# A gated attention kernel on one Trainium2 core: the attention phase with every engine and the DMA queue held to the order of the source

## Chip, cores and metric

The kernel runs on one core of one Trainium2 chip. The metric is the device time of one execution in microseconds (us), as the median of several runs. Five engines work side by side: TensorE (PE in the profile; its weight loads are PEld), VectorE (DVE), ScalarE (ACT), GpSimd (POOL) and SyncE (SP). Each works through its own list of instructions in order and waits on semaphores for the others. Transfers are issued from the lists of SP, ACT or POOL.

## What is computed

Eight sequences x (512 tokens of 256 features, float32) pass four blocks, each added to x with a scalar gate tanh(g), and each reading a layernorm of x:

```
x = x + tanh(g0) * cell(ln(x), ctx, ctx)        # mLSTM cell, 8 heads of 32
x = x + tanh(g1) * ffn0(ln(x))                  # attention, 32 heads of 8, then experts
x = x + tanh(g2) * cross(ln(x), ctx)            # attention, 16 heads of 16, key mask
x = x + tanh(g3) * ffn1(ln(x))                  # product-key experts, 8 heads, top 8 of 4096
```

The cell weighs its scores with exp of cumulated gates, causally. `ffn0` is softmax attention within a sequence, a projection, and for each 256-token half of a sequence one of eight two-layer gelu experts; `cross` is softmax attention over the context. `ffn1` projects, normalises over the whole batch, picks the best keys, and sums gelu(x . down) * weight * up over the chosen experts; the kernel takes the products with all 4096 rows of `down` and picks afterwards.

## The kernel before, in words

There are three phases. The **attention phase** (`attention_phase`) does the first three blocks for all sequences, and next to them the products with `down` for `ffn1`. The short **fold** prepares the key matrix. The **chosen phase** (`chosen_phase`) does the picking and sums; its lists of PE, DVE, ACT and POOL are written by hand.

In the attention phase one Python driver decides the order of PE's list, and a scheduler that sits between the kernel's source and the chip orders the lists of all other engines and of SP by its own estimate. The driver is `run` (line 264). It keeps a `Clock` (line 36): a guess of when PE, DVE, ACT and POOL are done with what has been written so far. In each turn it collects candidates, each with the time from which it may run, takes the first that is ready, or else the earliest, and lets it write its instructions.

* **Half-steps** (`attend`, `half_step`). The two attentions are 48 jobs: 4 of kind A (`ffn0`) and 2 of kind C (`cross`) for each sequence. A job has 8 steps of two half-steps. One half-step writes score products (`sc`, L545) of the job whose row maxima are sought, and together with them score products of the job before it, whose exponentials are taken. DVE reduces the first to maxima (`nm`, L565), ACT takes exp of the second (`pr`, L601 for A, L604 for C). After a step PE multiplies `pr` with the values (`av`, L620). There are two score tiles, so the next half-step waits for DVE's nm and ACT's exp of the one before. 48 jobs x 16 half-steps, with maxima and exponentials side by side, make 768.
* **Slots** (`fill_slot`, L507). Before a job, queries and keys are read from images in DRAM (`im_Aq` and so on, written by `halve`, L459 and L460) into one of three slots: 32 transfers for a job of kind A, 24 for one of kind C, and 4 more of a mask row for each second job of kind C. All are issued on SP.
* **Lane 1** per sequence m: load of X and cT (L304, L306, POOL's queue), `cell` (layernorm `qn`, gates, four pairs of heads; for each pair a broadcast load `mb` of 512 KB, L756, masked by POOL at L775, turned into `pd` by ACT at L784, multiplied by DVE at L798 with the scores `csc`, L791, and summed by PE into `cav`, L766), `queries`, `values0` and `context` (images and values for the jobs).
* **Lane 2** per sequence: `experts` (w1e, w2e and b2e loaded on POOL's queue, L671 to L689; products L940 and L967; gelus L954), `operands`, and after the jobs of kind C `leave`, which stores x and its layernorm and frees X.
* **The down lane** (`inner_products`): for each sequence, once it has left, 32 pieces of four products (`ps_hd`, L209), evacuated to `raw` by ACT or DVE and stored to DRAM.

Candidates of `attend` come first in the list, then lane 2, lane 1 and the down lane; so a lane runs where no half-step, tail or value product is ready. Lane pieces that need PSUM share two banks (`Room`, line 153). A lane ends a piece with `yield t`, the time at which it wants to go on; `("rest", name)` waits for an event, and `("take", ...)` for the one accumulator that cell and experts share. `stats`, `normalize` and `layernorm` (lines 117 to 139) write all of their DVE instructions in one go, and POOL's inverse square root between them.

## Time and profile before

| | us |
|---|---|
| three runs | 4493.82, 4502.52, 4508.36 |
| median | 4502.52 |
| profiled execution, its own time | 4506.63 |
| its span | 4504.9 |
| PE, PEld, DVE, ACT, POOL busy | 3811.9, 2039.0, 2482.6, 1777.3, 773.2 |
| mean granted clock of TensorE | 0.84 |
| first and last nm of a half-step fall into | 160 to 450, 3150 to 3375 |
| last down products and fold | 3375 to 3495 |
| chosen phase | 3495 to 4505 |

The profile is one execution. A busy PE is not PE at its peak: its matrix products are pipelined, and they take about twice the time where the granted clock is 0.5. The idle time of an engine is put down to the one whose semaphore came last.

### The profile page before, as it was taken

The numbers are of one execution on the slowest core, as the hardware profiler recorded it, in microseconds if no ns is written. First come the engines' busy times: TensorE is split into PE (matmuls) and PEld (weight loads), VectorE is DVE, ScalarE is ACT, GpSimd is POOL, SyncE is SP. The second block draws the span as 40 slices with busy tenths as digits, with TensorE's granted clock in tenths as the row PEclk, the third lists the DMA queues.
The fourth block names the chain that finished last, engine by engine and source line by source line (L and its number), as shares of the span: only waits on it lengthen the run. The fifth ranks groups of instructions, "written<-read, shape, count | busy, mean of one in ns | idle before, by whom it ended". The sixth has DMA issues, their size and how long they took to land.

```text
span 4504.9 us, 60683 instructions
## 1 busy us (share of the span) xinstructions
PE 3811.9 (85%) x23237; PEld 2039.0 (45%) x23237; DVE 2482.6 (55%) x5698; ACT 1777.3 (39%) x2382; POOL 773.2 (17%) x998
## 2 busy tenths in 40 slices
PE   5587888789879887997899789898898688888888
PEld 2233434333433442353334334433434466666667
DVE  2555533454445444544443454433332899999997
ACT  2244534354534544453445345444441323322321
POOL 2110100100011001101000100100000444444443
PEclk7677857788878977997888889796898799999999
DMA  2311311223233222332332232231255022222221
GB/s 88 83 50 45 80 40 45 66 87 99 73 79 94 87 68 85 103 82 57 104 94 64 78 92 82 67 117 33 78 173 189 32 84 75 90 89 72 87 88 48
DMA packets 206227, 365.81 MB, mean 81 GB/s; under 512 B 27376, under 2 KB 150544, under 8 KB 201456
## 3 DMA queue, kind: packets, MB, share of 16 engines
q1 hardware_dynamic: 187008, 304.99, 22.2%
q0 software_dynamic: 13824, 48.24, 3.7%
q10 hardware_dynamic: 5104, 8.69, 0.5%
q8 instruction: 184, 3.01, 0.3%
q14 instruction: 107, 0.88, 0.1%
HBM read 248.43 MB, written 113.39 MB: 80 GB/s over the span
## 4 chain that ended last, share of the span: by engine, by line
PE 34%; DVE 24%; ACT 3%; DMA 2%; issue 2%; POOL 2%; SPq 0%; ACTq 0%; POOLq 0%; DVEq 0%
PE sc L545 10%; PE ps_hd L209 8%; PE av L620 5%; DVE m L1466 4%; DVE m L1479 4%; DVE g L1508 3%; DVE nm L565 2%; DVE i L1331 2%; PE ps_p L426 2%; PE ps_y L967 2%; DVE s L1329 2%; PE ps_h L940 1%; ACT pr L604 1%; ACT pr L601 1%; DVE ppk L1331 1%
## 5 line engine op out<-in xcount | busy, mean ns | idle before, releaser
L565 DVE TENSOR_REDUCE nm<-sc 128x2 f32<-128x1024 f32 x768 | 937.8, 1223 | 1117.4 <-PE sc L545 1114.1
L601 ACT ACTIVATE pr<-sc 128x1024 f32<-128x1024 f32 x512 | 523.3, 1022 | 605.7 <-PE sc L545 586.0
L545 PE MATMUL sc<-ks,qs 32*128 32x512 f32 x1536 | 490.6, 580 | 101.1 <-DVE nm L565 74.1
L209 PE MATMUL ps_hd<-dx,dw 128*128 128x512 f32 x1024 | 535.4, 656 | 36.8 <-DMA dx<-xT_d 19.2
L545 PEld LDWEIGHTS sc<-ks,qs 32*128 32x128 f32 x1536 | 187.6, 210 | 687.1 <-issue 382.4
L1516 PE MATMUL acc<-up_sb,g 128*128 128x256 f32 x2048 | 476.8, 386 | 2.1 <-issue 2.1
L545 PE MATMUL sc<-qs,ks 32*128 32x512 f32 x1536 | 422.0, 545 | 36.8 <-DVE nm L565 32.4
L604 ACT ACTIVATE pr<-sc,m_off 128x1024 f32<-128x1024 f32 x256 | 282.6, 1113 | 354.8 <-PE sc L545 354.2
L1516 PEld LDWEIGHTS acc<-up_sb,g 128*128 128x128 f32 x2048 | 381.3, 191 | 63.6 <-issue 15.6
L620 PE MATMUL av<-pr,va 128*32 128x512 f32 x2048 | 336.8, 736 | 75.4 <-ACT pr L601 73.4
L1487 POOL TENSOR_TENSOR m<-m2b,wr 64x512 bf16<-64x512 bf16 x256 | 270.5, 1057 | 521.0 <-DVE m L1479 502.9
L545 PE MATMUL sc<-mx,pick_g 4*128 4x512 f32 x1536 | 353.1, 452 | 0.0
L209 PEld LDWEIGHTS ps_hd<-dx,dw 128*128 128x128 f32 x1024 | 189.9, 203 | 269.9 <-issue 235.8
L176 ACT COPY raw<-ps_hd 128x512 f32<-128x512 f32 x204 | 118.8, 584 | 332.4 <-PE ps_hd L209 316.1
L1499 PE MATMUL cf<-m,m 128*128 128x64 bf16 x6144 | 230.7, 200 | 14.3 <-POOL m L1487 10.6
L1499 PEld LDWEIGHTS <-m 128*128 128x128 bf16 x6144 | 226.2, 103 | 30.3 <-issue 11.5
L620 PE MATMUL av<-pr,vb 128*32 128x512 f32 x1024 | 162.8, 713 | 61.4 <-ACT pr L604 61.4
L671 POOL DMA_DIRECT2D w1e<-in_w x32 | 23.3, 728 | 1069.5 <-PE ps_h L940 1069.5
L545 PEld LDWEIGHTS sc<-qs,ks 32*128 32x128 f32 x1536 | 169.6, 211 | 78.2 <-DVE nm L565 42.1
L775 POOL TENSOR_SCALAR_AFFINE_SELECT mb<-mb 128x256 f32<-128x256 f32 x128 | 52.2, 407 | 876.0 <-DMA mb<-nM_d 484.0
L784 ACT ACTIVATE pd<-mb,aT 128x512 f32<-128x512 f32 (+3 forms) x256 | 131.2, 555 | 180.6 <-PE cav L766 82.6
L1466 DVE TENSOR_TENSOR m<-ml,iota 128x2048 bf16<-128x2048 bf16 x128 | 195.2, 1525 | 0.0
(232 smaller groups left out, 5656.4 us busy)
## 6 DMA issues: line engine op xcount, KB each, us to landing
g_d<-raw SPq DMA_DIRECT2D x128, 512.0 KB
g<-g_d SPq DMA_DIRECT2D x32, 2048.0 KB
dw<-in_down SPq DMA_DIRECT2D x128, 256.0 KB
w1e<-in_w POOLq DMA_DIRECT2D x32, 512.0 KB, 4.2
w2e<-in_w POOLq DMA_DIRECT2D x32, 512.0 KB, 4.6
mb<-nM_d SPq DMA_DIRECT2D x32, 512.0 KB
qs<-im_Aq SPq DMA_DIRECT2D x512, 32.0 KB
ks<-im_Ak SPq DMA_DIRECT2D x512, 32.0 KB
```

Source lines behind the costliest of these rows:

```text
L209: nc.tensor.matmul(ps.tile, dws[i][:, k, u, :], xt[:, k, :], start=(k == 0), stop=(k == NK - 1),)
L545: nc.tensor.matmul(sc[:, i, :], lhs[r : r + rows], rhs[r : r + rows], start=(n == 0), stop=(n == len(terms) - 1),)
L565: nc.vector.tensor_reduce(self.nm[:, c, 2 * half : 2 * half + 2, g], sc, AX.X, ALU.max, negate=True)
L601: nc.scalar.activation(self.pr[jj], sc, AF.Exp, scale=self.scale)
L604: nc.scalar.activation(self.pr[jj], sc, AF.Exp, bias=m_off[:, col : col + 1], scale=self.scale,)
L620: nc.tensor.matmul(self.av[32 * j : 32 * j + 32, :], self.va[:, c, h * (self.hd + 1) : h * (self.hd + 1) + 32], pr[j // 2][:, j % 2, :], s ...
L1331: last = nc.vector.max_index(out=index[:, n, :], in_max=values[:, n, :], in_values=source(n))
L1466: nc.vector.tensor_tensor(m1, at[:, 0].unsqueeze(2).to_broadcast([P, 8, P, 2]), iota.unsqueeze(1).to_broadcast([P, 8, P, 2]), ALU.is_equal,)
L1479: last = nc.vector.tensor_tensor(m2[r, 0:2, :, NJ * d : NJ * d + NJ, :], m2b[r].unsqueeze(1).to_broadcast([64, 2, 8, NJ, 2]), wr[r, u, 0:2 ...
L1487: after(nc.gpsimd.tensor_tensor(m2[r, 2, :, NJ * d : NJ * d + NJ, :], m2b[r], wr[r, u, 2].unsqueeze(2).to_broadcast([64, 8, NJ, 2]), ALU.mult,
L1499: nc.tensor.matmul(cf[:, s, :], m1[:, s // 2, :, s % 2], m2[:, i, s // 2, :, s % 2], start=(i == 0), stop=(i == 2),)
L1516: nc.tensor.matmul(accs[t], gts[t][:, j, :], up_sb[:, j, :], start=(j == 0), stop=(j == NJ - 1))
```

## The change

All five lists of the attention phase (PE, DVE, ACT, POOL, SP) follow the order in which the driver writes the instructions; the scheduler no longer moves any of them. With that the helpers are cut: a new `("side", t)` yield marks a place between two pieces that need no PSUM bank; such pieces are put ahead of everything else that is ready. The driver's times get somewhat longer (0.65 for 0.5 for four transposes, 0.14 more a half-step, 0.08 more for a value product). Transfers issued on POOL's queue are issued on SP's. The setup of constants that PE and POOL began with becomes a lane, `prepare`. The `cell` writes `decay` two blocks ahead of the scores. Images have three buffers, and `values1` is a piece of its own that lane 2 writes after `leave` for sequences 2 and up. Two rules pace the lanes: each half-step adds 1.42 us of credit for lane work on PE, and lane pieces come ahead of the next half-step as long as credit is left; and the down lane is held to a line from 0 pieces at 28% of the half-steps to 195 at their end, ahead of the other lanes when more than 3 pieces behind it, and after the half-steps when not behind it.

The core of the diff (the other places do the same to their lines: `nc.gpsimd.dma_start` becomes `nc.sync.dma_start` for X, cT, w1e, w2e, b2e and cte; callers of the helpers use `yield from`; `side` yields stand between the gate computations):

```diff
+        self.work = 0.0
         self.at = {"dve": 0.0, "act": 0.0, "pool": 0.0}
 
     def mm(self, cost, after=0.0):
         self.pe = max(self.pe, after) + 1.08 * cost
+        self.work += 1.08 * cost
         return self.pe + 0.3
 
...
 
+    def side(t):
+
...
         for c in range(NC):
             nc.vector.bn_stats(st[:, c, :], src[:, c, :])
+            t = ck.on("dve", 0.42, after)
+            if c % 2:
+                yield side(t - 0.5)
         for c in range(NC):
             nc.vector.bn_aggr(mv[:, c, :], st[:, c, :])
+        t = ck.on("dve", 0.6, after)
         inv_sqrt(rs, mv[:, :, 1], EPS_LN)
-        return mv, rs, ck.on("dve", 2.2, after)
+        t = ck.on("pool", 1.5, t)
+        yield side(t)
+        return mv, rs, t
...
+            t = ck.on("dve", 0.4, after)
+            if c % 2 and c < NC - 1:
+                yield side(t - 0.5)
+        return t
...
+            t = self.at if self.side else max(self.at, room())
+            if self.need is not None and (self.need == "prepared" or self.need[1] >= 0):
                 if self.need not in done:
...
+                elif said[0] == "side":
+                    self.side, self.at = True, said[1]
...
-    def run(lanes, others=lambda: []):
+
+    SHARE = 1.42
+    pace = {"credit": 0.0, "part": 0.0, "down": 0}
+
+    def behind():
+
+        return 195 * max(0.0, pace["part"] - 0.28) / 0.72 - pace["down"]
+
+    def run(lanes, down, others):
+
+
+        def piece(lane):
+            def step():
+                before = ck.work
+                lane.step()
+                pace["credit"] -= ck.work - before
+                if lane is down and ck.work > before:
+                    pace["down"] += 1
+
+            return step
 
         while True:
-            cands = others()
+            first, half = [], []
+            for t, step, is_half in others():
+                (half if is_half else first).append((t, step))
+            rest = []
             for lane in lanes:
                 t = lane.when()
                 if t is not None:
-                    cands.append((t, lane.step))
+                    (first if lane.side else rest).append((t, piece(lane)))
+            t = down.when()
+            if t is not None:
+                if behind() > 3:
+                    rest.insert(0, (t, piece(down)))
+                elif behind() > 0 or not half:
+                    rest.append((t, piece(down)))
+                else:
+                    spare = NJ * sum(("left", m) in done for m in range(M)) - pace["down"]
+                    rest.append((max(t, ck.pe + max(0.1, 0.8 - 0.05 * spare)), piece(down)))
+            cands = first + (rest + half if pace["credit"] > 0 else half + rest)
...
-            nc.gpsimd.dma_start(xbs[m], x[b].rearrange("(c p) d -> p c d", p=P))
+            nc.sync.dma_start(xbs[m], x[b].rearrange("(c p) d -> p c d", p=P))
             cTs[m] = cxp.tile([P, NK, S], F32, name="cT", tag="cT")
-            nc.gpsimd.dma_start(cTs[m], cxT[b].rearrange("(k p) s -> p k s", p=P))
+            nc.sync.dma_start(cTs[m], cxT[b].rearrange("(k p) s -> p k s", p=P))
 
...
-        nc.gpsimd.memset(nms.bitcast(F32), 0.0)
...
-        nc.gpsimd.memset(cte, 1.0)
-        for i in range(2):
-            nc.gpsimd.memset(v0s[i], 1.0)
-            nc.gpsimd.memset(v1s[i], 0.0)
-
+        nc.vector.memset(cte, 1.0)
...
-        bo_ps = ps_m.tile([P, S], F32, name="bo_ps", tag="m")
-        for k in range(NK):
-            nc.tensor.matmul(
-                bo_ps[:, :D], bqkv_sb[:, 4 + k : 5 + k].to_broadcast([P, P]), w3_sb[:, 3, k, :],
-                start=(k == 0), stop=(k == NK - 1),
-            )
-        nc.vector.tensor_tensor(tbo, bo_ps[:, :D], tbo, ALU.add)
-        nc.vector.tensor_scalar(tbo, tbo, tg[:, 2:3], None, ALU.mult)
...
+        def prepare():
+
+            yield side(ck.pe + 12.0)
+            for i in range(2):
+                nc.vector.memset(v0s[i], 1.0)
+                yield side(ck.dve(NC * W0 // 2, ck.pe) + 0.5)
+            nc.gpsimd.memset(nms.bitcast(F32), 0.0)
+
+            nc.vector.tensor_reduce(p2, ident.rearrange("p (m g) -> p g m", g=2), AX.X, ALU.add)
+            nc.vector.tensor_copy(pick, p2)
+            yield side(ck.on("dve", 0.5, ck.pe) + 1.0)
+            nc.sync.dma_start(m_u8, mask)
+            yield side(ck.pe + 4.0)
+            m_f = prb.tile([P, 2, S], F32, name="m_f", tag="pr")[: B * NC, 0, :P]
+            nc.vector.tensor_copy(m_f, m_u8)
+            t = ck.on("dve", 0.3, ck.pe)
+            m_neg = prb.tile([P, 2, S], F32, name="m_neg", tag="pr")[: B * NC, 0, :P].bitcast(F32R)
+            nc.vector.tensor_scalar(m_neg, m_f, 1.0, -NEG, ALU.subtract, ALU.mult)
+            nc.sync.dma_start(m_dram, m_neg.bitcast(F32))
+            yield t
+            mp = Room([P, S], "mp", t)
+            nc.tensor.transpose(mp.tile[:, : B * NC], m_f, ident[: B * NC, : B * NC])
+            mp.mm(0.2)
+            nc.vector.tensor_copy(m_key, mp.tile[:, : B * NC])
+            mp.free(ck.on("dve", 0.3, mp.t))
+            nc.vector.tensor_scalar(m_off, m_key, 1.0, -NEG, ALU.subtract, ALU.mult)
+            ck.on("dve", 0.3, mp.t)
+            yield ck.pe + 4.0
+            bo_ps = Room([P, S], "bo_ps")
+            for k in range(NK):
+                nc.tensor.matmul(
+                    bo_ps.tile[:, :D], bqkv_sb[:, 4 + k : 5 + k].to_broadcast([P, P]),
+                    w3_sb[:, 3, k, :], start=(k == 0), stop=(k == NK - 1),
+                )
+            bo_ps.mm(NK * D * F4)
+            nc.vector.tensor_tensor(tbo, bo_ps.tile[:, :D], tbo, ALU.add)
+            bo_ps.free(ck.dve(D, bo_ps.t))
+            nc.vector.tensor_scalar(tbo, tbo, tg[:, 2:3], None, ALU.mult)
+            yield side(ck.dve(D, bo_ps.t) + 2.0)
+            for i in range(2):
+                nc.gpsimd.memset(v1s[i], 0.0)
+                yield side(ck.on("pool", 2.0, ck.pe) + 2.0)
+            done["prepared"] = ck.pe
...
+            t = ck.act(S, ps.t)
+            ps.free(t + 1.5)
+            yield side(t)
+            if bias is None:
                 nc.vector.tensor_tensor(lo, ps.tile, hi.bitcast(F32), ALU.subtract)
             else:
-                nc.scalar.activation(hi, ps.tile, AF.Identity, bias=bias)
-                t = ck.act(S, ps.t)
                 nc.vector.scalar_tensor_tensor(
                     lo, ps.tile, bias, hi.bitcast(F32), ALU.add, ALU.subtract
                 )
-            ps.free(ck.dve(S, t))
+            t = ps.free(ck.dve(S, t))
             nc.sync.dma_start(dst[0, n], hi.bitcast(F32))
+            yield side(t)
             nc.sync.dma_start(dst[1, n], lo.bitcast(F32))
...
-            images[(kind, m)] = drm.tile([2, 2, P, S], F32, name=f"im_{kind}")
+            images[(kind, m)] = drm.tile([2, 2, P, S], F32, name=f"im_{kind}", bufs=3)
...
-            def close_maxima(self):
+            def gather_maxima(self):
                 at = nms.rearrange("p c (j r) -> p c j r", j=4)
                 nc.vector.tensor_copy(at[:, :, :, 0:2], self.nm)
                 nc.vector.tensor_tensor(
                     at[:, :, :, 2:4], self.nm, at[:, :, :, 0:2].bitcast(F32), ALU.subtract
                 )
-                t = ck.on("dve", 0.3, self.reduced)
-                ps = Room([P, S], "nmT", t)
+                self.gathered = ck.on("dve", 0.4, self.reduced)
...
+            def close_maxima(self):
+                ps = Room([P, S], "nmT", self.gathered)
...
-                t = ck.mm(S * F4, there)
+                t = ck.mm(S * F4 + 0.08, there)
...
-                nc.gpsimd.dma_start(
+                nc.sync.dma_start(
...
+            yield side(ck.pe + 2.5)
             for pair in range(4):
                 mb = cel.tile([P, 2, S], F32, name="mb", bufs=1)
                 nc.sync.dma_start(mb, nM_d[2 * pair : 2 * pair + 2].partition_broadcast(P))
-                yield ck.pe + 4.5
+                yield side(ck.pe + 3.0)
...
+                def decay(c):
                     s0 = c * P
                     nc.gpsimd.affine_select(
...
-                    t = ck.on("pool", 0.5, ck.pe)
-                    pd = cel.tile([P, 2, S], F32, name="pd")
+                    t = ck.on("pool", 0.8, ck.pe)
+                    pd = pds[c] = cel.tile([P, 2, S], F32, name="pd")
...
+                    ready[c] = t
+
+                def scored(c):
+                    s0 = c * P
+                    pd = pds[c]
...
@@ -799,12 +874,29 @@
                             pd[:, i, s0:], sc[i].tile[:, s0:], 1.0 / math.sqrt(32.0),
                             pd[:, i, s0:], ALU.mult, ALU.mult,
                         )
-                        t = sc[i].free(ck.dve(S - s0, max(t, sc[i].t)))
-                    if last is not None:
-                        sums(*last)
-                    last = (c, pd, t)
-                    yield 0.0 if c < NC - 1 else t
-                t = sums(*last)
+                        ready[c] = sc[i].free(ck.dve(S - s0, max(ready[c], sc[i].t)))
+
+                def sums(c):
+                    pd = pds.pop(c)
+                    for i in range(2):
+                        h = 2 * pair + i
+                        nc.tensor.matmul(
+                            av[64 * i : 64 * i + 64, c * P :],
+                            cte[:, c, 33 * h : 33 * h + 64],
+                            pd[:, i, c * P :], start=(c == 0), stop=(c == NC - 1),
+                        )
+                    return ck.mm((S - c * P) * F4, ready[c])
+
+                decay(0)
+                yield side(ready[0] - 1.0)
+                decay(1)
+                for c in range(NC):
+                    yield ready[c] - 0.5
+                    scored(c)
+                    yield ready[c]
+                    t = sums(c)
+                    if c + 2 < NC:
+                        decay(c + 2)
                 avs = osb.tile([P, S], F32, name="avs", tag="avs", bufs=1)
                 nc.scalar.copy(avs, av)
                 t = ck.act(S, t)
...
-                t = ht.free(ck.on("dve", 1.2, ht.t))
-            t = layernorm(hk, hk, t)
+                t = ht.free(ck.on("dve", 1.4, ht.t))
+                yield side(t)
...
-            yield ("rest", ("loaded", m - 2, 3, "A"))
+            yield ("rest", ("loaded", m - 3, 3, "A"))
...
-            yield ("rest", ("job", m - 2, 1, "C"))
+
+        def values1(m):
+            b = order[m]
+            yield ("rest", "prepared")
+            cT = cTs[m]
...
-            yield tp
+            yield side(tp - 3.5)
...
+                yield side(max(t, tb))
...
                 yield from context(m)
+                if m < 2:
+                    yield from values1(m)
...
                 yield from leave(m)
+                if m + 2 < M:
+                    yield from values1(m + 2)
...
-                    def close(job=job):
-                        closed[job] = live[job].close_maxima()
-                        st["close"] = None
-                    cands.append((max(live[job].reduced + 0.3, room()), close))
+                    op = live[job]
+                    if op.gathered is None:
+                        cands.append((op.reduced, op.gather_maxima, False))
+                    else:
+                        def close(job=job):
+                            closed[job] = live[job].close_maxima()
+                            st["close"] = None
+                        cands.append((max(op.gathered, room()), close, False))
...
-            t = ck.mm(deep * S * F1)
+            t = ck.mm(deep * S * F1 + 0.14)
+            pace["credit"] = min(pace["credit"] + SHARE, 2 * SHARE)
+            pace["part"] = st["i2"] / (STEPS * len(jobs))
...
-        lanes = [Lane(lane2()), Lane(lane1()), lane_down]
-        run(lanes, attend)
+        lanes = [Lane(lane2()), Lane(lane1()), Lane(prepare())]
+        run(lanes, lane_down, attend)
...
-    with tc.manual_schedule(engines={mybir.EngineType.PE}):
+    with tc.manual_schedule(
+        engines={
+            mybir.EngineType.PE, mybir.EngineType.DVE, mybir.EngineType.Activation,
+            mybir.EngineType.Pool, mybir.EngineType.SP,
+        }
+    ):
```

## The prediction, made before the changed kernel ran

> **What bounds the kernel now.** I read the page's slices first, then the table of stages, then TensorE's waits, then the timelines of single stops. The profiled execution took 4506.63 us with a span of 4504.9 us; the median of the three runs, 4502.52 us, lies 4 us lower, so sums against the span are lowered by 2.4 us at the end.
>
> ```profile
> PE   5587888789879887997899789898898688888888
> DVE  2555533454445444544443454433332899999997
> PEclk7677857788878977997888889796898799999999
> ```
>
> The last ten slices are the chosen phase: DVE is full there, and the change doesn't touch it (3495 to 4505, 1010 us). The first thirty are the attention phase and the short fold. There no other engine is full: TensorE is busy 8 or 9 tenths of the time, but its granted clock swings between 0.6 and 0.9. The stages, as start:end, us, busy us of PE, PEld, DVE, ACT and POOL, granted clock, DMA share, GB/s:
>
> ```profile
> 160.00:450.00 290.00, 224.63 (x1060) 88.32 (x1060) 161.07 (x262) 118.58 (x165) 24.41 (x45) 0.69 0.22 56
> 450.00:900.00 450.00, 370.83 (x1876) 185.57 (x1872) 193.28 (x283) 195.57 (x225) 55.62 (x64) 0.74 0.21 58
> 900.00:1350.00 450.00, 389.80 (x1957) 172.95 (x1956) 210.76 (x321) 207.64 (x266) 43.41 (x62) 0.84 0.30 85
> 1350.00:1800.00 450.00, 392.66 (x2008) 175.52 (x2008) 208.97 (x324) 207.00 (x268) 44.20 (x64) 0.84 0.29 84
> 1800.00:2250.00 450.00, 394.70 (x2032) 181.23 (x2028) 210.42 (x331) 208.31 (x270) 43.81 (x63) 0.86 0.30 86
> 2250.00:2700.00 450.00, 393.35 (x1970) 180.34 (x1968) 207.50 (x340) 199.53 (x256) 47.63 (x65) 0.83 0.29 82
> 2700.00:3150.00 450.00, 407.72 (x2100) 189.03 (x2098) 182.72 (x226) 205.16 (x241) 21.93 (x26) 0.82 0.26 74
> 3150.00:3375.00 225.00, 204.90 (x1120) 101.74 (x1120) 72.89 (x117) 100.64 (x122) 10.82 (x13) 0.93 0.38 122
> ```
>
> These 3215 us hold all 768 half-steps. PE is busy 2778.6 us in sum, so it idles 436 us. Each stage's busy time by its clock gives the work at full clock: 155.0 + 274.4 + 327.4 + 329.8 + 339.4 + 326.5 + 334.3 + 190.6 = 2277 us. The other 501 us of busy time are lost to the low clock. So the stage runs at 2277 / 3215 = 71% of what PE could do, and 937 us are in play. The waits of PE in it (total, times, longest):
>
> ```profile
> PE sc L545 <- DVE nm L565: 106.5, 118, 6.6
> PE ps_t L403 <- DVE qn L132: 77.9, 5, 17.8
> PE av L620 <- ACT pr L601: 73.4, 83, 2.3
> PE av L620 <- ACT pr L604: 61.4, 64, 1.4
> ```
>
> The clock goes with them. Around one wait for qn and in a stretch where the lanes had no work left, the same table reads:
>
> ```profile
> 2101.00:2119.00 18.00, 3.37 (x14) 0.89 (x11) 1.77 (x9) 1.02 (x1) 6.46 (x8) 0.50 0.26 73
> 2119.00:2129.00 10.00, 9.62 (x32) 4.17 (x32) 4.35 (x7) 2.19 (x3) 0.00 (x0) 0.55 0.01 2
> ...
> 3045.00:3056.00 11.00, 7.63 (x59) 2.81 (x57) 4.60 (x5) 4.37 (x6) 0.00 (x0) 1.00 0.31 93
> ...
> 3070.00:3120.00 50.00, 40.87 (x201) 16.22 (x200) 17.50 (x18) 15.53 (x17) 0.00 (x0) 0.50 0.04 11
> ```
>
> After the stop PE works 10 us at half clock. From 3045 on there are only half-steps and values. PE first gets by with 7.63 of 11 us; then the clock falls to 0.50 and stays, with 41 of 50 us busy: a pair of half-steps that took 5.2 us takes 7.2 us in the timeline. So missing filler costs the gap and then the clock.
>
> **The change part by part.** No matrix product is added, so the 2277 us stay; what changes is who waits.
>
> *Loads of X, cT, cte, w1e, w2e, b2e go from POOL's queue to SP's.* At 2110 the load of X stands behind POOL's work for another sequence:
>
> ```profile
> 2109.12 0.91 POOL L923 TENSOR_SCALAR b2e<-b2e,tg 128x256 f32<-128x256 f32 x1 [2.73 <-DMA b2e<-in_b]
> ...
> 2110.77 0.77 POOL L304 DMA_DIRECT2D X<-in_x  x1
> 2115.75 1.41 DVE L123 BATCH_NORM_STATS2 ln_st<-X 128x6 f32<-128x256 f32 x4 [15.04 <-DMA X<-in_x]
> ```
>
> DVE sits in front of its next nm for 15 us, PE with it. On SP the load goes out where lane 1 asks for it, 5 us by the driver before its first reader; its issue-to-landing median is 4.8 us. I count the 77.9 us as gone. What is late next there is the chain statistics, POOL, normalisation, about 6 us, under half-steps. SP pays for 128 more issues at 0.34 us (an mb issue) to 0.9 us (a cte issue on POOL): 44 to 115 us of its own time in 3000, on no path unless something urgent stands behind.
>
> *DVE, ACT, POOL in the order of the source, helpers cut by side yields.* At 1869 to 1875 DVE ran bn_stats, aggregates, two waits of 1.47 us for POOL and four normalisations before one nm whose scores were ready, and PE stood 5.73 us. With the cuts a half-step's nm can go in between. Of the 106.5 us I take half, 53: the 118 waits average 0.9 us, and the short ones are plain latency. The bounds are 0 and 106. The gelus of an expert half are written together: before, 63 table loads at L954 for 32 halves, 55 at L604 and 13 at L601, 1283 ns each; about half go, some 80 us of ACT, which is busy under half of the time, so nothing by itself.
>
> *Credit of 1.42 us a half-step, and the down lane held to a line.* Lane pieces then stand between exponentials and values. Of the 134.8 us of av waits I take half, 67; of the waits for gates (16.7 + 4.0 us), 10. The bounds are again nothing and all. The down products (L209) are missing from 1577-1689, 2365-2477, 2815-2928 and 3040-3153, with clocks of 0.76, 0.81, 0.77 and 0.70 against 0.94 in the slices beside them: (0.18 x 97.5) + (0.13 x 101.6) + (0.17 x 99.3) + (0.24 x 95.2) = 70 us. Spread to 195 pieces over the last 72% they fill these; I take 50, since part is in the next term.
>
> *The new in-order waits.* No row shows them. The nearest: a fill of one A job's slot is 32 SP issues, from 1522.30 to 1537.37, that is about 12 us without its wait, and mb (needed by POOL, then ACT, then the exponentials behind it) can stand behind one. Fills take 48 x 12 = 576 us, a fifth of SP's time, and the mean rest of one is 6 us: 28 loads of mb beside half-steps x 0.2 x 6 = 34 us. With a like share for DVE and ACT I take 60; the ends are 0 and 28 x 12 = 336.
>
> *Start.* PE waits 11.14 us for mp and 18.92 us for bo_ps, and DVE's tbo holds the first layernorm behind it: the first transposes come at 33.62. With `prepare` later they need X and about 6 us of chain: 20 us gained. Three images and values1 in lane 2 only move work; nothing taken. The tail (3375 to 3495: last down, fold) is kept at 120 us.
>
> **The sum.** Idle: -78 - 53 - 67 - 10 + 60 = -148, leaving 288 of 436. The clock's loss follows idle in proportion: 501 x 148 / 436 = -170, and -50 for the down lane. Start: -20. Together -388: 4504.9 - 388 = 4117 us of span, 4115 against the median. The stage then runs at 2277 / (3215 - 368) = 80%; the old kernel's stretch 2690-2810 reaches 106.91 x 0.93 / 120 = 83% and 1465-1577 84%, so this asks for nothing unseen.
>
> Two rules of the Trainium skill speak against parts of this. "TensorE: Matmul & The Clock Gate", section "Why this matters for your kernels", asks only for no idle gaps over about 3 us; yet the stretch at 3070 has none above 0.8 us and stays at 0.50. By the rule only five stops would give clock back (5 x 5 us), not 220 us, and the time would be about 4310; I go by the row. "DMA: Bandwidth & Descriptors", section "Issuing engines are not separate DMA queues", says that the issuing engine saves only sequencer time; what the row at 2110 shows is that sequencer's queue, 12 us of it. By the rule alone the X term falls and the time is some 170 us higher.
>
> **Rivals.**
> 1. *The order hardly differs, or latency is the limit.* For it: most PE waits are under 1 us, and PE was in the driver's order already. Then only the X loads (78 us + 5 x 5 us of clock) and the start (20) go: 4505 - 123 = 4380.
> 2. *SP's single queue stalls the exponentials; slower.* The place is mb behind fills and behind waits for buffers. For it: POOL already waits 484.0 us in 30 pieces for mb, up to 40.3 us, and SP stands 560.9 us at L507 for slots. Against it: those waits cost ACT only 50.2 us, as its order had other work first, and a fill is now issued when the driver says its slot is free. A stop of 12 us costs 12 + 5 of clock; 28 of them 476 us: 4115 + 476 = 4591. It decides once the mean stop passes about 10 us (28 x 14 = 390).
> 3. *The balance starves the lanes*, so that jobs wait for images: a cell alone takes 33 to 111 us at the start; 30 us of that exposed in each of seven sequences takes 210 us back: 4325, still faster.
>
> **How the numbers follow.** Forecast (3880 to 4335, rival 3 in it) 0.66, and 0.04 below; rival 1 (4335 to 4490) 0.10; within 0.3% of 4502, which is about what a measurement tells from no change, 0.03; rival 2 and its like 0.17. The lower end is the best: 2277 / 0.88 = 2587, 628 us less, and 20: 3857, rounded to 3880. The range takes in rival 1 and ends at 4520, leaving out 0.04 below and some 0.15 above. The forecast's own range is 3880 to 4335.
>
> **What would show it.** Right: no wait for qn above 3 us; granted clock near 0.9 in all stages after 450; L209 in every slice from about 0.28 on; few av waits; the last half-step near 2960 instead of 3349. Wrong: ACT pd or POOL mb waits that stand right before PE's stops; DVE waiting for POOL or DMA with nm behind; slices at clock 0.7 that hold L209; or a chosen phase other than 1010 us.

## The result, and the profile after

The kernel after takes 4529.76 us (median of 13 runs, 4512.56 to 4576.2), the kernel before 4495.56 us beside it (13 runs, 4467.67 to 4508.36): ratio 1.008, interval [1.0052, 1.0108]. It is slower, a little; 4115 us were forecast. The profiled execution took 4512.56 us, the fastest of the 13, with a span of 4510.8 us.

In the slices, the full ones at the end are as before. In the first thirty TensorE shows as many sevens and eights as it did:

```profile
PE   5587889889779889987888999788887689888888
PEclk6656869789889788996988989687898799999999
```

The stages of the kernel after (start:end, us, busy us of PE, PEld, DVE, ACT and POOL, granted clock, DMA share, GB/s), some of them, and then the whole stretch:

```profile
160.00:450.00 290.00, 221.55 (x944) 87.23 (x944) 136.85 (x224) 98.80 (x127) 23.56 (x37) 0.62 0.22 51
...
900.00:1350.00 450.00, 377.11 (x1941) 175.35 (x1939) 205.22 (x322) 188.42 (x244) 30.10 (x44) 0.89 0.32 90
1350.00:1800.00 450.00, 402.58 (x2016) 180.40 (x2016) 210.88 (x331) 196.81 (x256) 31.86 (x48) 0.84 0.29 84
...
2700.00:3150.00 450.00, 370.25 (x1904) 175.09 (x1900) 168.59 (x218) 176.65 (x214) 24.95 (x27) 0.80 0.25 72
```

```profile
160.00:3375.00 3215.00, 2736.98 (x14090) 1262.14 (x14090) 1459.52 (x2249) 1341.26 (x1709) 221.20 (x308) 0.83 0.28 80
```

PE idles 3215 - 2737 = 478 us here, where it idled 436. Busy time by clock, stage by stage, is 2278 us: the same work in the same 3215 us, with 459 us lost to the clock in place of 501. The waits of PE (total, times, longest), from the start to the chosen phase:

```profile
PE sc L615 <- DVE nm L635: 141.4, 116, 24.5
PE av L692 <- ACT pr L673: 83.8, 86, 1.2
PE ps_hd L224 <- DVE pd L873: 49.5, 26, 10.0
PE sc L615 <- ACT pr L673: 48.0, 38, 11.1
```

L635 is the nm of L565 before, L615 the scores, L692 the values. The waits for qn are gone (1.6 us in this stretch after 77.9). In their place stand long stops at nm, pd and pr: between 160 and 3375 there are 16 stops of 4 us or more, 174 us in all, where the kernel before had 14 with 134 us. One of 24.47 us ends at 2049.74. SP's list ahead of it:

```profile
2002.78 6.25 SPq L576 DMA_DIRECT2D qs<-im_Aq  x16
2009.30 6.56 SPq L576 DMA_DIRECT2D ks<-im_Ak  x16
2016.00 6.21 SPq L576 DMA_DIRECT2D qs<-im_Aq  x16
2022.25 7.17 SPq L576 DMA_DIRECT2D ks<-im_Ak  x16
2029.77 7.32 SPq L576 DMA_DIRECT2D qs<-im_Aq  x16
2037.23 7.19 SPq L576 DMA_DIRECT2D ks<-im_Ak  x16
2044.60 0.34 SPq L527 DMA_DIRECT2D im_Ck<-pk_h  x1
2045.04 0.38 SPq L529 DMA_DIRECT2D im_Ck<-pk_l  x1
```

and what the other engines do when it is through (the bracket: idle time before, and what ended it):

```profile
2047.08 0.69 ACT L516 ACTIVATE pk_h<-ps_p,bqkv_sb 128x512 fp32r<-128x512 f32 x1 [35.50 <-DMA im_Ck<-pk_h]
2047.80 0.75 DVE L523 SCALAR_TENSOR_TENSOR pk_l<-ps_p,bqkv_sb,pk_h 128x512 fp32r<-128x512 f32 x1 [26.68 <-ACT pk_h L516]
...
2049.74 0.79 PE L615 MATMUL sc<-ks,qs 32*128 32x512 f32 x2 [24.47 <-DVE nm L635]
```

Read upwards: PE waits for an nm, which stands in DVE's list behind a pk_l; that needs a pk_h of ACT; ACT waits 35.5 us for a free pk_h buffer, because the store that frees it (L527) stands in SP's list behind three slot fills. Those are 96 issues and last 42 us. Each piece is where the driver wrote it. The same thing with mb in the place of the store stops PE for 8.81 us at 981.67, behind one fill of kind C that keeps SP from 961.68 to 974.24; here the way leads over POOL's mask and pd:

```profile
970.58 3.66 SPq L576 DMA_DIRECT2D kx<-im_Ck  x8
974.66 0.34 SPq L836 DMA_DIRECT2D mb<-nM_d  x1
...
979.73 0.41 POOL L845 TENSOR_SCALAR_AFFINE_SELECT mb<-mb 128x256 f32<-128x256 f32 x1 [36.01 <-DMA mb<-nM_d]
980.17 1.34 ACT L854 ACTIVATE pd<-mb,aT 128x512 f32<-128x512 f32 x2 [10.85 <-POOL mb L845]
```

And the load of X, which the change put on SP, is itself caught once, behind two fills and four stores:

```profile
164.93 5.37 SPq L576 DMA_DIRECT2D ks<-im_Ak  x16
...
172.25 0.77 SPq L353 DMA_DIRECT2D X<-in_x  x1
178.75 0.75 DVE L129 BATCH_NORM_STATS2 ln_st<-X 128x6 f32<-128x256 f32 x2 [16.44 <-DMA X<-in_x]
...
180.68 0.79 PE L615 MATMUL sc<-ks,qs 32*128 32x512 f32 x2 [17.52 <-DVE nm L635]
```

Sorted by the transfer that comes late, the 174 us are: image stores 66.5 us (three stops of 21 to 24 us), mb or the store nM_d that it reads 55.7 us (six of 7 to 11), X 17.5 us (one), the fills' own keys 22.4 us (four of 5 to 7) and dw, the rows for the down products, 12.2 us (two).

### The profile page after: what moved, and what is told of

The parts are those of the page before. It is cut to its first block, busy times and chain, and to the rows that moved or that the text cites. A ratio compares the mean times of both kernels' runs of the same rounds, so it can differ in the third digit from the quotient of the medians.

```text
span 4510.8 us, 60390 instructions
## 1 busy us (share of the span) xinstructions
PE 3775.1 (84%) x23237; PEld 2027.6 (45%) x23237; DVE 2501.0 (55%) x5742; ACT 1675.8 (37%) x2279; POOL 670.4 (15%) x867
## 5 line engine op out<-in xcount | busy, mean ns | idle before, releaser
L635 DVE TENSOR_REDUCE nm<-sc 128x2 f32<-128x1024 f32 x768 | 934.8, 1222 | 992.9 <-PE sc L615 983.8
L615 PE MATMUL sc<-ks,qs 32*128 32x512 f32 x1536 | 487.2, 587 | 200.8 <-DVE nm L635 138.8
L224 PE MATMUL ps_hd<-dx,dw 128*128 128x512 f32 x1024 | 535.9, 653 | 99.8 <-DVE pd L873 49.5
L615 PEld LDWEIGHTS sc<-ks,qs 32*128 32x128 f32 x1536 | 188.9, 212 | 708.5 <-issue 292.9
L615 PE MATMUL sc<-qs,ks 32*128 32x512 f32 x1536 | 398.7, 536 | 33.1 <-ACT pr L673 24.6
L692 PE MATMUL av<-pr,va 128*32 128x512 f32 x2048 | 347.3, 757 | 84.5 <-ACT pr L673 83.8
L615 PE MATMUL sc<-mx,pick_g 4*128 4x512 f32 x1536 | 335.8, 446 | 0.0
L191 ACT COPY raw<-ps_hd 128x512 f32<-128x512 f32 x171 | 100.3, 587 | 299.9 <-PE ps_hd L224 289.5
L873 DVE SCALAR_TENSOR_TENSOR pd<-csc,pd 128x512 f32<-128x512 f32 (+3 forms) x256 | 115.3, 487 | 167.4 <-PE csc L866 110.1
L615 PEld LDWEIGHTS sc<-qs,ks 32*128 32x128 f32 x1536 | 159.5, 206 | 102.9 <-issue 46.6
L116 POOL TENSOR_SCALAR ln_rs<-ln_mv 128x4 f32<-128x4 f32 x40 | 9.3, 232 | 1211.5 <-DVE ln_mv L134 1211.5
```

The costliest lines, as they stand in the source:

```text
L224: nc.tensor.matmul(ps.tile, dws[i][:, k, u, :], xt[:, k, :], start=(k == 0), stop=(k == NK - 1),)
L615: nc.tensor.matmul(sc[:, i, :], lhs[r : r + rows], rhs[r : r + rows], start=(n == 0), stop=(n == len(terms) - 1),)
L635: nc.vector.tensor_reduce(self.nm[:, c, 2 * half : 2 * half + 2, g], sc, AX.X, ALU.max, negate=True)
L692: nc.tensor.matmul(self.av[32 * j : 32 * j + 32, :], self.va[:, c, h * (self.hd + 1) : h * (self.hd + 1) + 32], pr[j // 2][:, j % 2, :], s ...
```

## The experiments

The theory to test, S: the cost lies in SP's list, where urgent small transfers stand behind fills of 24 to 32 issues. Its rivals are named at each run. Every ratio is to the kernel before, run beside it on the same chip; the kernel before took 4490 to 4499 us in these, so medians of different runs can be set side by side to some 10 us.

**Fewer issues for a fill** (e1), and the same in the kernel before (e3). A fill becomes 8 or 6 transfers of the same bytes, with the rows of the two halves interleaved in the slot; the sum over rows doesn't mind their order.

```diff
-                    for j in range(4):
-                        at = 32 * j + h * u
-                        nc.sync.dma_start(
-                            dst[at : at + h].rearrange("d g s -> d (g s)").bitcast(F32),
-                            src[half, n, r + 2 * h * j : r + 2 * h * (j + 1)].rearrange(
-                                "(d g) s -> d (g s)", g=2
-                            ),
-                        )
+                    nc.sync.dma_start(
+                        dst[u :: len(halves)].rearrange("d g s -> d (g s)").bitcast(F32),
+                        src[half, n, r : r + 8 * h].rearrange("(d g) s -> d (g s)", g=2),
+                    )
```

> The changed kernel, but a slot is filled with 8 transfers for a job of kind A in place of 32, and 6 for one of kind C in place of 24: the rows of a slot are interleaved (partition 4d+u in place of 8u+d, the same for queries and keys, so the products stay the same), and each transfer covers all four row groups. Same bytes. Theory S (urgent transfers stand behind bursts of slot issues on SP's one list): PE's stops of 4 us and more after SP's bursts go, 20.9 + 17.5 + 24.5 + 21.1 (pk_l and nm), 37.4 (pd), 18.3 (pr), 12.2 (dw), 30.6 (ks) = 182 us, and up to as much again in clock: 4170 to 4350. Theory P (the pacing does not spread the lanes, the queue is a side matter): within 1% of 4530.

> The kernel before with the same slot transfers as e1_merge. It stopped only once for a slot (10.1 us), and its scheduler moves urgent transfers ahead. S and P: 4440 to 4500, a gain of at most 1%. If it gains as much as e1_merge does against the changed kernel, then the number of issues costs by itself and not by what stands behind them.

e1: 4307.05 us, ratio 0.9581 [0.9552, 0.961]. Between 160 and 3250 us four stops of 4 us or more are left, 35.5 us, and the longest of them (20.0 us, for dw) lies behind the last half-step. S held. (The 182 us of stops that this expectation and that of e7 name are the 174 us above; the keys, ks, have 22.4 us and not 30.6.) e3: 4335.59 us, 0.9657 [0.962, 0.9694], where at most 1% was expected: a miss. There the waits for qn went from 77.9 us to none while those for nm (106.4) and values (139) stayed as they were. So in the kernel before, too, the many issues did harm; by which way isn't shown, since the scheduler reorders its lists when the fills change.

**SP's list, or all but PE's, left to the scheduler** (e2, e4): `mybir.EngineType.SP` or all but `mybir.EngineType.PE` taken out of the set at the end of the phase.

> The changed kernel with SP's list given back to the scheduler, the other four held to the source. S: the scheduler puts mb and the image stores ahead of slots, so most of the long stops go, 4350 to 4450. P: 4530, within 1%.

> The changed source with only PE's list held to it, as before; all else is ordered by the scheduler. It separates the new source (pieces, pacing, SP as issuer) from the held lists. S: the held SP list is what costs, so 4300 to 4450. P: the pacing is what fails, so 4500 to 4600.

e2: 4359.19 us, 0.9686 [0.9651, 0.9722], in S's range, but only half of the stops went: 7 with 91 us are left, as the scheduler too puts a fill and more ahead of image stores (ACT waits 18.2 us for a pk_h at 1939.46). e4: 4464.53 us, 0.9938 [0.9915, 0.996], between S's range and the rival's; the new source is not itself slower when PE alone is held. Side by side the two part the held lists: with the new source, to hold DVE, ACT and POOL as well gains 105 us (4464.53 to 4359.19), and to hold SP's list too costs 171 us (4359.19 to 4529.76).

**More issues, and another queue** (e8, e7). Each transfer cut in two by rows; and

```diff
-            nc.sync.dma_start(dst[0, n], hi.bitcast(F32))
+            nc.gpsimd.dma_start(dst[0, n], hi.bitcast(F32))
...
-            nc.sync.dma_start(dst[1, n], lo.bitcast(F32))
+            nc.gpsimd.dma_start(dst[1, n], lo.bitcast(F32))
...
-                nc.sync.dma_start(mb, nM_d[2 * pair : 2 * pair + 2].partition_broadcast(P))
+                nc.gpsimd.dma_start(mb, nM_d[2 * pair : 2 * pair + 2].partition_broadcast(P))
```

> The kernel after, with each slot transfer cut in two: 64 and 48 issues for a fill in place of 32 and 24, the same bytes to the same places. Theory S (the number of issues in SP's list is the price): taking 24 of 32 away gave 223 us, so 32 more for each fill cost 180 to 360 us, 4710 to 4890 us, with POOL's wait for mb longer than the 55 us mean of the kernel after, and stops at pk_l and nm of 35 to 45 us in place of 21 to 24. Theory B (the form of the merged transfer, its bytes or its landing, was what gained, not the count): within 1% of 4530 us.

> The kernel after, with the block-maximum load mb and the two image stores of each half head issued on POOL's queue and not on SP's; the slot fills stay 32 and 24 transfers on SP. Theory S (what costs is that these few urgent transfers stand behind a fill in SP's list): the stops of 21 to 24 us at pk_l and nm, 84 us in all over four heads, the pd stops that follow a late mb (37 us) and the pr stops that follow the same (18 us) go, 139 of the 182 us in stops of 4 us or more, and with the clock that comes back 4330 to 4430 us. Theory P (the order of PE's list and the pacing cost, the queue does not): within 1% of 4530 us. Theory F (the fills are late for themselves, whatever stands behind them): the stops at ks, qs stay and grow, and less than 60 us is gained, 4470 to 4540 us.

e8: 4759.14 us, 1.0599 [1.0574, 1.0624], as S expected. (The 55 us named there are POOL's longest wait for mb in the kernel after and not the mean; here it is 63.3.) The stops grow with the issues; this one follows three fills of 64, and the chain ahead of it is the one shown above:

```profile
2199.35 0.69 ACT L516 ACTIVATE pk_h<-ps_p,bqkv_sb 128x512 fp32r<-128x512 f32 x1 [58.75 <-DMA im_Ck<-pk_h]
...
2202.12 0.80 PE L618 MATMUL sc<-ks,qs 32*128 32x512 f32 x2 [40.15 <-DVE nm L638]
```

With 8, 32 and 64 issues for a fill of kind A the same source takes 4307, 4530 and 4759 us. e7 leaves the 32 and takes the small transfers out of their way: 4365.86 us, 0.9727 [0.9696, 0.9758]. SP still issues three fills in a row from 1136.41 to 1176, but the stores go out of POOL's list meanwhile at 0.54 us each, and PE doesn't stop there. This too is as S expected: it is the place in the list, not the transfers' landing. Seven stops with 69 us are left in e7, and three of them have the same cause, small transfers that e7 left on SP: one of 18.3 us at 176.43 waits for X behind a fill, and the two for pd (8.3 and 8.9 us) for an mb that waits in POOL's list for the store nM_d, behind a fill on SP (the other four wait for dw):

```profile
1249.56 5.65 SPq L576 DMA_DIRECT2D ks<-im_Ak  x16
...
1255.37 0.26 SPq L814 DMA_DIRECT2D nM_d<-nM  x1
...
1258.17 0.63 POOL L836 DMA_DIRECT2D mb<-nM_d  x1 [49.12 <-DMA nM_d<-nM]
...
1265.53 2.93 PE L224 MATMUL ps_hd<-dx,dw 128*128 128x512 f32 x3 [8.33 <-DVE pd L873]
```

**Everything held, with the old source** (e5), and that with short fills (e12): in the kernel before, the engine set of the kernel after.

> The source of the kernel before (its planner, its pieces, its 32-transfer fills), with all five engines and queues held to the order of that source, not PE's alone. Theory S: the fills stand ahead of the urgent transfers in SP's list here too, and without the small side pieces DVE's statistics also hold up nm: 4550 to 4750 us, with qn waits gone (78 us in the kernel before, below 5 us here) and stops at pk_l, mb and nm of 15 us or more. Theory P (what costs is the new planner): as the kernel before or faster, 4380 to 4500 us.

> The source of the kernel before with all five lists held to its order, and merged fills. With 32-transfer fills that kernel took 4409 us and had one stop over 8 us between 160 and 3250 us. Theory S (fewer issues gain only through the stops that they make in SP's list): little is left to gain, 4330 to 4410 us. Theory B (the count costs everywhere, also through transfers that land later or a clock that drops): 4200 to 4270 us, as far below as with the other sources (160 to 223 us).

e5: 4408.91 us, 0.9812 [0.9787, 0.9838]. S was wrong here and the rival right: holding all five lists is no loss with the old source but gains 81 us. It has one stop over 8 us between 160 and 3250 us. In its list the stores mostly stand ahead of the fills (im_Aq to im_Ck from 2197.15 to 2223.05, the next fill from 2234.37), and after the start fills seldom come in a row. e12: 4368.38 us, 0.9733 [0.9682, 0.9785]: only 41 us are gained by short fills where no urgent transfer stands behind them, as S expected. So S is right about the mechanism, and what brings it about must be in the new source.

**What in the new source?** Part (a) of the change undone (e10): `nc.gpsimd.dma_start` again for X, cT, cte, w1e, w2e and b2e, the lists held.

> The kernel after with part (a) of the change undone: X, cT, the cell's columns, expert weights and their biases are again issued on POOL's queue, in the source's order like everything else. Theory Q (in SP's list these loads wait for a free weight buffer, 421 us on PE ps_h in the kernel after, and hold up the fills and stores behind them): 4400 to 4470 us. Theory S (it is the fills' own issues that hold up the rest): within 1% of 4530 us.

4498.83 us, 1.0037 [1.0008, 1.0066]: 31 us better than the kernel after by medians, 19 us by the ratios, whose intervals overlap. The stops at pk_l and nm behind image stores (19 to 21 us) and at pd stand as before; the one of 17.5 us at the start is gone, as X no longer stands behind the fills (14 stops, 150 us). So it is a small part and not the cause. PE's wait for qn is 1.6 us here too, though X is back on POOL's queue.

The pacing rules taken out, with short fills (e9), with 32 issues (e6), and one by one (e13 the credit, e14 the down lane's line):

```diff
-                if behind() > 3:
-                    rest.insert(0, (t, piece(down)))
-                elif behind() > 0 or not half:
-                    rest.append((t, piece(down)))
-                else:
-                    spare = NJ * sum(("left", m) in done for m in range(M)) - pace["down"]
-                    rest.append((max(t, ck.pe + max(0.1, 0.8 - 0.05 * spare)), piece(down)))
-            cands = first + (rest + half if pace["credit"] > 0 else half + rest)
+                rest.append((t, piece(down)))
+            cands = first + half + rest
```

> The kernel after with merged fills (8 and 6 transfers), and with the planner's two pacing rules taken out: lanes are tried in the old order (attention's own, then its other half, then the rest), and a down piece is offered as soon as it is ready. If the pacing is worth nothing, as the slices of the kernel after say, where the down lane stops in six places all the same: within 1% of the 4307 us of merged fills alone. If the balance does what it is for: 4350 to 4450 us, with the down lane used up early and the nm stops back in the stretches without it. If it harms (rival 3 of the prediction): 4200 to 4270 us.

> The kernel after, 32-transfer fills, with only the planner's two pacing rules taken out (lanes tried in the old order, down pieces offered as soon as ready). Theory L (the pacing makes the lanes late, so that the images of the next block are complete only when two or three slots are already free and their fills stand on SP back to back, 42 us of issues): about the 4409 us of the old planner with all lists held, 4370 to 4450 us, with the stops of 20 us at pk_l and nm gone. Theory S alone (pacing worth nothing, as the 9 us between the two merged kernels say): within 1% of 4530 us, stops as before.

> The kernel after, 32-transfer fills, with only the credit rule taken out: where the attention's half steps and the other lanes can both start, the half step goes first again; the down lane keeps its line. If the credit is what makes the fills of a block stand together with the image stores behind them: most of the 136 us that both rules cost, 4380 to 4440 us. If it is the down lane's rule: 4490 to 4560 us.

> The kernel after, 32-transfer fills, with only the down lane's rule taken out: a down piece is offered like any other lane's piece, the credit stays. If the down lane's line is what costs: 4380 to 4440 us. If it is the credit: 4490 to 4560 us. If each does half: 4440 to 4490 us in both kernels.

| fills, pacing | us | ratio to before | stops of 4 us or more, 160 to 3250 |
|---|---|---|---|
| 32, both rules (after) | 4529.76 | 1.008 [1.0052, 1.0108] | 16, 174 us |
| 32, no credit (e13) | 4418.5 | 0.9829 [0.9809, 0.9849] | 13, 121 us |
| 32, no line for the down lane (e14) | 4444.72 | 0.9887 [0.986, 0.9915] | 14, 120 us |
| 32, neither (e6) | 4393.55 | 0.98 [0.9746, 0.9854] | 12, 92 us |
| 8, both (e1) | 4307.05 | 0.9581 [0.9552, 0.961] | 4, 36 us |
| 8, neither (e9) | 4298.45 | 0.9571 [0.9536, 0.9605] | 1, 18 us |

With 32 issues the two rules cost 136 us together; taking out either one gives back most of it (111 and 85 us), so neither is the cause alone, and each of the two expectations that named one rule fell. With 8 issues they cost and gain nothing. In e6 the fills still come three in a row at 1191.76 (to 1228), but the four Cq stores are ahead of them and only Ck's behind; in the kernel after all eight stand behind (first store at 1241.41 after fills from 1197.58). The longest stop of e6, 22.4 us at 182.38, is X's again. That is the way seen; how the two rules together arrive at it in the driver's bookkeeping I have not followed.

**Together** (e11: e1 and e7; e15: e1, e7 and e9).

> The kernel after with merged fills (8 and 6 transfers) and also mb and the image stores on POOL's queue. Theory S: both edits take away the same stops, so little is left for the second, 4270 to 4310 us beside 4307 for merged fills alone. If they gain for different reasons (223 and 164 us): 4140 to 4200 us.

> All three edits that gained, together: merged fills, mb and the image stores on POOL's queue, both pacing rules out. Theory S (one set of stops, which merged fills take nearly whole): 4265 to 4300 us, within 1% of the 4277 us without the third edit. If the gains of the pacing rules' removal (136 us at 32 transfers) were of another kind: below 4200 us.

e11: 4276.9 us, 0.9555 [0.9503, 0.9608]. e15: 4276.37 us, 0.951 [0.9494, 0.9526], 4.9% below the kernel before and 5.6% below the one after by medians. The gains don't add: 223 and 164 us apart give 253 together, and the pacing then nothing. They remove mostly the same stops. The stretch of e15 that ends where its half-steps have long been through, and PE's waits over the run up to the chosen phase:

```profile
160.00:3135.00 2975.00, 2702.24 (x14084) 1245.50 (x14082) 1451.69 (x2243) 1339.01 (x1709) 301.10 (x452) 0.85 0.26 86
```

```profile
PE sc L605 <- DVE nm L625: 75.4, 102, 3.2
PE av L682 <- ACT pr L663: 74.2, 74, 1.6
PE tr L1541 <- DVE mlw L1527: 46.8, 8, 10.1
PE av L682 <- ACT pr L666: 42.8, 51, 1.4
```

No wait for nm is longer than 3.2 us, and pk_l and pd are gone from the head of the list. 125 short waits for values, 117 us in all, remain.

## Why the prediction was wrong, step by step

* **"The new in-order waits … I take 60": the step that failed first.** It named mb behind one fill of 12 us and took a mean rest of 6 us, 34 us in all, and 26 us more for all else. The stops of 4 us or more sum to 174 us: mb has 56 of them, and the longest have other carriers and a longer queue, the image stores behind up to three fills (42 us), through ACT's pk_h buffers and DVE's pk_l to nm. What makes these long is fills back to back, which the prediction didn't consider. To take the stops away is worth 164 us (e7), 223 us (e1) or 253 us (e11) of time. With the clock that the sum put on idle, its 60 us stood for 129 us of time (60 x 2.15), so without the term it would have said 3986 us; e11, whose half-steps have no such stop left, takes 4277. Of the 415 us between forecast and measurement some 125 are thus this term, and some 290 are gains that didn't come, which are the next points.
* **Rival 2** had the sign and the queue, and its price, 17 us for a stop of 12 (1.4 for one), is near what the runs show: 223 us of time for 139 us of stops (e1), 164 for 105 (e7), 1.6 for one. Its 4591 counts part twice, as the 4115 from which it starts holds the 129 us already.
* **"Credit … held to a line": gain -77 and -50, measured a loss.** The rules cost 136 us with these fills and nothing with short ones. The waits for values fell from 134.8 to 113.3 us, a third of the 67 taken, and the rules didn't do even that: e15 without any rule has 117.0, and e5, the old source with its lists held, 116.4. The down lane is not spread. PE's busy tenths of its products in 40 slices, kernel before and then after:

```profile
busy tenths in 40 slices 0000000034014103300320231070157000000000
```

```profile
busy tenths in 40 slices 0000000043034004201410420250167000000000
```

 Between the first and the last products seven slices are empty in both. The line asks for 195 pieces over the last 72%, but 32 pieces come at a time, when a sequence has left, and while 14 or more are spare the rule holds one back by only 0.1 us of the driver's time (`max(0.1, 0.8 - 0.05 * spare)`). I read the line and not this exception; that it is what keeps the slices empty is read from the source, and no run takes it out alone.
* **"The clock's loss follows idle in proportion" (-170): mis-sized.** In the kernel after idle rose by 42 us and the clock's loss fell by 42. e15 reaches the forecast's idle almost exactly, 2975 - 2702 = 273 us where 288 were summed; its work at full clock by stages is 2310 us (a little of the tail's down products is in it), so 392 us are lost to the clock, and 281 were forecast. That is 109 us for 163 us of idle, 0.67 for one, where the sum took 1.15 and 50 more for the down lane. All of these come from one profile of each kernel. Since the 288 held 60 us of the new waits and e15 has none of them, the forecast without that term would have been 228 us of idle and 212 us lost to the clock (501 - 1.15 x 208 - 50): of the 290 us above some 180 are the clock's.
* **Loads of X (-78): size right, reason not needed.** The waits went (1.6 us). But they are 1.6 us in e10 as well, with X on POOL's queue, and 8.0 in e5, whose source is the old one: the held order, which puts the load where the source wrote it, is enough. (Short fills are too, none is left in e3; and in e4, with X on SP and only PE held, the wait is 0.3 us.) The price of the queue was put at nothing "unless something urgent stands behind"; the loads themselves stood behind the fills, 17.5 us at the start, and cost some 20 to 30 us by e10.
* **nm (-53): the gain has another cause.** Three stops at nm (17.5, 24.5 and 21.1 us) make up 63 of the 141.4 us after. The other 78 and the 75.4 of e15 are some 30 less than 106.5. It isn't the side yields that took them: e5, which has none, waits less than either, and e4, which has them but leaves DVE's list to the scheduler, waits more than the kernel before. The held order did it. First e5, then e4:

```profile
PE sc L545 <- DVE nm L565: 67.0, 108, 2.6
PE sc L615 <- DVE nm L635: 122.0, 133, 2.9
```

* **Start (-20): nearly right.** The first nm starts at 150.2 where it started at 167.7, 17.5 us earlier (160.7 in e5, which has no `prepare`), and the stop for X at 180.68 takes as much away again.
* **ACT's table loads (some 80 us of ACT): right.** The 131 in attention became 71 (32 for gelu, 28 and 11 for the exponentials), 77 us less, and as forecast that alone shows nowhere.
* **Chosen phase, 1010 us: right**; its first product starts at 3503.1 (3495.6 before), and it takes 1008 us of the profiled execution.

Of the signs set down, "right" were the qn waits alone; the clock, the slices with down products and the last half-step (its nm starts at 3299.0 after 3311.9) were not. The sign set down for "wrong" that came is pd waits right before PE's stops, as rival 2 has them: the 49.5 us above. Two small readings of the lines were off, without weight in the sum: the clock's digits go down to 5, not 6, and the stretch at 3070 has one gap of 1.04 us, at 3115.69.

The two pages weighed against the sum fared so. "DMA: Bandwidth & Descriptors" of the Trainium skill, section "Issuing engines are not separate DMA queues", says that issuing from several engines saves only time on the sequencer, usually small beside the transfer. It is that time which e7 takes out of the way of the small transfers; for three fills in one in-order list it was 42 us, and the run was 164 us shorter: not small here. The same page, section "Rules for kernel authors", advises to join small transfers, below 64 KB above all; the transfers of a fill of kind A grow from 32 to 128 KB in e1 and the time agrees (223 us), but where nothing urgent is behind them the same edit gave 41 us (e12). "TensorE: Matmul & The Clock Gate", section "Why this matters for your kernels", asks for no idle gap over some 3 us. e15 has no stop above 2.5 us between 160 and 3135 us and still loses 392 us to the clock, so the rule alone doesn't restore it; as the weighing said, long stops were not the whole of it, but I had made the clock follow all idle too closely.

**Open**: why short fills gain 160 us in the kernel before; how the two pacing rules bring the fills together; why the clock's loss follows idle so loosely; and which of its sides makes the new source with short fills (4307) 61 us better than the old one held in the same way (4368).

## What to carry to other kernels

Before the order of a DMA queue is fixed, count the issues that stand ahead of each small transfer that something waits for, bursts of bulk transfers included, and ask also who needs the buffer that a store frees; then make the bulk transfers few, or put the small ones on another queue. Read a pacing rule with its exceptions and with how its supply arrives. Don't price a clock in proportion to idle time: take it from two profiles of the same code where there are any, and keep its bounds apart.

## What was not expected of the hardware

* What a bulk transfer costs in a list goes with its number of issues more than with its bytes: 16 issues of 32 KB took 6.2 to 7.3 us (about 0.4 us each), while 4 of 128 KB, the same bytes, took 2.39 to 2.60 us in e1 (0.6 us each). A fill of kind A is so 5 us of SP's list in place of 13 to 15, with the same bytes.
* At nearly the same work the clock's loss moved by 0.67 us for a us of idle (e15 against before) and once the other way (42 us more idle and 42 us less lost, after against before), so mean idle alone doesn't set it in these kernels.
